# Layer 2 of a four-layer graph kernel: phi1 applied to the features before the sum over neighbours, psi and phi1 taken from the turned h in three exact passes

## The chip, the cores and the metric

The kernel runs on one core of one Trainium2 chip, in one launch. The metric is device time in microseconds (us) from start to end of the execution. TensorE is called PE, VectorE DVE, ScalarE ACT, GpSimd POOL, and SP is the queue that issues nearly all DMAs. PEld is the loading of weights into PE, which overlaps its matmuls.

## The reference

The input is 32 samples (`x`: 32 x 512 nodes x 128 features, float32) with one 512 x 512 adjacency matrix. Four layers follow one another, each as `x = x + layer(relu(layernorm(x)))`. The change lies in layer 2:

```python
h = jnp.maximum(_layernorm(x, axis=-1), 0.0)
weights = coeff * A                       # both are adj here: adj squared
features = relu(einsum('bnd,de->bne', h, psi_w) + psi_b)
messages = einsum('nm,bnd->bmd', weights, features)
phi_in = concatenate((messages, h), axis=-1)
hid = relu(einsum('bnk,kd->bnd', phi_in, phi1_w) + phi1_b)
x = x + einsum('bnd,de->bne', hid, phi2_w) + phi2_b
```

`phi1_w` has 256 rows: the upper 128 meet the messages, the lower 128 meet `h`. Layer 3 is an attention with `tanh`, `exp` and a mask; layers 0 and 1 also mix over the nodes.

## The kernel before

All of `x` stays in SBUF, as 16 pairs of samples. For each sample of a layer, ACT writes the normalised `h` (four instructions of 128 x 128, `chunk`), DVE turns it in 32 x 32 blocks (`turn_half`), and SP sends each pair through DRAM and back (`fetch`), which gives `hT`: features on partitions, nodes along the free axis.

Precision: a product that must be exact in float32 is either a plain float32 matmul (two PE instructions in the profile) or three float32r matmuls of `high`, `low` and `mid` parts. The parts are made by `moving_parts` (ACT, POOL and DVE, from SBUF), `fixed_parts` (ACT, POOL, ACT, POOL, for weights) or `bank_parts` (ACT, then two DVE instructions, straight from a PSUM bank).

Layer 2 is a loop over the samples n = 0 to 31 in `layers_2_and_3`. Each engine works through its instructions in the order in which the program issues them; the order is written out by hand (a manual schedule), so the place of a call in the loop is its place in the queue of every engine it uses. Before the change, iteration n holds, in this order:

- `messages(n)`: 12 float32r matmuls of the feature parts with the squared adjacency (L1182), into bank `p_msgT`.
- `turn_ready`: DVE turns of the h that were written an iteration earlier (one of layer 2, one of layer 3 for n from 8 on), and their stores to DRAM.
- `chunk(3, ...)` for n from 7 on and `chunk(2, n + 7)` for n up to 24: ACT writes h of layer 3 and of layer 2 (L1133). So both come in iterations 7 to 24.
- a DVE scaling of `p_msgT` into `msgT` (L1319), and `biased(n)`: POOL adds `phi2_b` to x (L1209).
- `features(n + 2)`: psi as eight float32 instructions (`p_feat`, L454), bias on DVE (L1170), relu on ACT (L1171), and the three parts (L420 ACT `high`, L421 POOL `low`, L422 DVE `mid`).
- `hidden(n - 1)`: phi1 in float32, two instructions for h (L1191) and two for the messages (L1192), then ACT's relu (L1193).
- `updated(n - 2)`: phi2 in float32 (`p_l2`, in the profile `p_l<-phi,msgT`, L454), DVE adds it to x (L1201). After every second sample, `ln_stats` follows: four DVE statistics (L245), one ACT square root (L252), two short DVE instructions (L256, L257). They serve layer 3.
- in iterations 2 to 5 one more `ln_stats`, for the last pairs of layer 2 (ACT L254).

The last four steps of layer 1 (`mix`, PE line L1027) are interleaved with the first steps of layer 2 by `more(3)` to `more(7)`; there stand `features(0)` and `features(1)`.

`bank` hands out the 8 PSUM banks, `small_tile` 13 SBUF tiles of 128 x 512, `matrix_tile` 3 tiles of 128 x 4 x 512.

Of the kernel before, what the change touches and what calls it, by code (L numbers as in the profile page):

```python
# [9 lines left out]
F32 = mybir.dt.float32  # L10
F32R = mybir.dt.float32r
F16 = mybir.dt.float16
BF16 = mybir.dt.bfloat16
AF = mybir.ActivationFunctionType
# [3 lines left out]
P = 128  # L18
# [11 lines left out]
def kernel(  # L30
# [53 lines left out]
    def bank(name):  # L84
        return psum.tile([P, 512], F32, tag="bank", name=name)

    def tiles(ap):
        return ap.rearrange("p (t f) -> p t f", f=D)

    def blk(t):  # L90
        return slice(t * P, (t + 1) * P)
# [5 lines left out]
    def matrix_tile(name, dtype=F32):  # L97
        return const.tile([P, NT, N], dtype, tag="matrix", name=name, bufs=3)
# [4 lines left out]
    def small_tile(name, dtype=F32):  # L103
        return after.tile([P, N], dtype, tag="small", name=name, bufs=13)

    def crossed(ap):

        return ap.rearrange("p (a b c) -> p b a c", a=NT, b=NQR)

    def split(ap):  # L110
        return ap.rearrange("p (a b c) -> p a b c", a=NT, b=NQR)
# [25 lines left out]
    def load_rows(ap, name, pool=const):  # L137
        o = ap.shape[0] // P
        w = pool.tile([P, o, ap.shape[1]], F32, name=name, bufs=1)
        nc.sync.dma_start(w, ap.rearrange("(o f) g -> f o g", f=P))  # L140
        return w

    def load_bcast(ap, name, pool=const):
        w = pool.tile([P, D], F32, name=name, bufs=1)
        nc.sync.dma_start(w, bass.AP(tensor=ap.tensor, offset=ap.offset, ap=[[0, P], [1, D]]))
        return w

    def spread(w, n):
        return w[:, None, :].to_broadcast([P, n, D])
# [15 lines left out]
        load_x(b)  # L165
    th = load_rows(theta, "th")
    b1 = load_bcast(bias_l1, "b1")
    psi = load_rows(psi_w, "psi")[:, 0, :]
    psib = load_bcast(psi_b, "psib")
    phi1 = load_rows(phi1_w, "phi1")  # L170
    phi1b = const.tile([P, 1], F32, name="phi1b")
    nc.sync.dma_start(phi1b, phi1_b.rearrange("(p o) -> p o", o=1))
    phi2 = load_rows(phi2_w, "phi2")[:, 0, :]
# [235 lines left out]
    def three(name):  # L409
        return [small_tile(f"{part}_{name}", F32R) for part in PARTS]  # L410
# [7 lines left out]
    def moving_parts(x, high, low, mid):  # L418

        nc.scalar.activation(high, x, AF.Copy, scale=DOWN)  # L420
        nc.gpsimd.tensor_sub(low, x, high.bitcast(F32))  # L421
        nc.vector.scalar_tensor_tensor(mid, x, 1.0 / UP, high.bitcast(F32), OP.mult, OP.subtract)  # L422

    def fixed_parts(x, high, low, mid):

        nc.scalar.activation(high, x, AF.Copy, scale=DOWN)
        nc.gpsimd.tensor_sub(x, x, high.bitcast(F32))
        nc.scalar.activation(low, x, AF.Copy, scale=LOW)
        nc.gpsimd.tensor_sub(mid, high.bitcast(F32), low.bitcast(F32))
# [16 lines left out]
    def columns(xT):  # L446
        return lambda t: xT[:, blk(t)]

    def projected(name, *terms):

        p = bank(name)
        for t in range(NT):
            for i, (hT, w) in enumerate(terms):
                nc.tensor.matmul(p[:, blk(t)], hT(t), w, start=(i == 0),  # L454
                                 stop=(i == len(terms) - 1))
        return tiles(p)
# [701 lines left out]
    def hT_of(layer, n):  # L1158
        return hTs[layer, n // 2][:, :, n % 2, :]

    feats, msgT, keys, query, hvs, exs = {}, {}, {}, {}, {}, {}

    def features(n):

        if n >= B:
            return
        hT = hT_of(2, n)
        pf = projected(f"p_feat_{n}", (lambda t: hT[:, t, :], psi))
        feat = small_tile(f"feat_{n}")
        nc.vector.tensor_add(tiles(feat), pf, spread(psib, NT))  # L1170
        nc.scalar.activation(feat, feat, AF.Relu)  # L1171
        feats[n] = three(f"feat_{n}")
        moving_parts(feat, *feats[n])

    def messages(n):

        if n % 4 == 0:
            msgT[n // 4] = matrix_tile(f"msgT_{n}")
        p = bank(f"p_msgT_{n}")
        for part in range(3):  # L1180
            for t in range(NT):
                nc.tensor.matmul(p, feats[n][part][:, blk(t)], sq[part][:, t, :],  # L1182
                                 start=(t == 0 and part == 0), stop=(t == NT - 1 and part == 2))
        return p

    def hidden(n):

        if not 0 <= n < B:
            return
        msg, p = msgT[n // 4][:, n % 4], bank(f"p_phi1_{n}")  # L1190
        nc.tensor.matmul(p, phi1[:, 1, :], hT_of(2, n), start=True, stop=False)  # L1191
        nc.tensor.matmul(p, phi1[:, 0, :], msg, start=False, stop=True)  # L1192
        nc.scalar.activation(crossed(msg), split(p), AF.Relu, bias=phi1b)  # L1193

    def updated(n):

        if not 0 <= n < B:
            return
        q, b = divmod(n, 2)
        p = projected(f"p_l2_{n}", (columns(msgT[n // 4][:, n % 4]), phi2))  # L1200
        nc.vector.tensor_add(xt[q][:, b], p, xt[q][:, b])  # L1201
        if b == 1 and q < NQ - 1:
            ln_stats(q, low=True)
# [90 lines left out]
    def layers_2_and_3():  # L1294


        later, ready = iter(range(B)), [(2, 6)]

        def ahead_of_3():
            m = next(later, B)  # L1300
            if m < B:
                chunk(3, m)
                ready.append((3, m))

        def turn_ready(now):
            for layer, m in now:
                turn_half(layer, m)

        mask_of = adjT_d.rearrange("(a b c) w -> b a c w", a=NT, c=QR)
        for n in range(B):  # L1310
            p = messages(n)
            turn_ready(ready)
            ready = []
            if 7 <= n < B - 1:
                ahead_of_3()
            if n + 7 < B:
                chunk(2, n + 7)
                ready.append((2, n + 7))
            nc.vector.tensor_scalar(msgT[n // 4][:, n % 4], p, UP, None, OP.mult)  # L1319
            biased(n)  # L1320
            features(n + 2)
            if n == B - 1:
                queries(0)
            hidden(n - 1)
            updated(n - 2)
            if n == 0:
                fetch(2, 2)
            elif n % 2 and n + 5 < B:
                fetch(2, n // 2 + 3)
            if n in (2, 3, 4, 5):  # L1330
                ln_stats(NQ - 6 + n)
            if n == 12:
                weights_of_3()
            if n == 20:
                adjTx.append(matrix_tile("adjTx"))
            if n >= 20 and n % 2 and n < 28:
                i = (n - 20) // 2
                tc.keep_in_program_order(nc.sync.dma_start(adjTx[0][:, i, :], mask_of[i]))
            if n in (26, 28, 30):
                fetch(3, (n - 26) // 2)  # L1340
            if n in (29, 30):
                key_parts(n - 29)
        key_parts(2)
        hidden(B - 1)
        mapped(0)
        updated(B - 2)
        updated(B - 1)
        for n in range(B):
            last = n == B - 1
            queries(n + 1)  # L1350
            if n:
                key_parts(n + 2)
            if n == 1:
                low_stats(NQ - 1)
            if last:
                attended(n - 2, NT // 2)
            else:
                scores(n)
                if n == B - 2:
                    attended(n - 1, 0, NT // 2)  # L1360
                    mapped(n + 1)
                    scores(n + 1)
                    continue
            attended(n - 1)
            mapped(n + 1)
            if n % 2:
                turn_ready(ready)
                ready = []
            elif n:
                ahead_of_3()  # L1370
            if n % 2 == 0:
                fetch(3, n // 2 + 3)
        attended(B - 1, width=1)
# [27 lines left out]
    def more(step):  # L1401

        if step == 0:
            chunk(2, 0)
            chunk(2, 1)
        elif step == 1:
            turn_half(2, 0)
        elif step == 2:
            turn_half(2, 1)
            fetch(2, 0)  # L1410
        elif step == 3:
            chunk(2, 2)
        elif step == 4:
            turn_half(2, 2)
            chunk(2, 3)
        elif step == 5:
            turn_half(2, 3)
            fetch(2, 1)
            features(0)
            chunk(2, 4)  # L1420
        elif step == 6:
            features(1)
            turn_half(2, 4)
            chunk(2, 5)
        elif step == 7:
            turn_half(2, 5)
            chunk(2, 6)
# [45 lines left out]
```

## Time and profile before

| | before |
|---|---|
| median of 3 runs | 905.54 us (905.1 to 905.81) |
| the profiled execution, its own time | 905.41 us |
| its span, first to last instruction | 903.6 us |
| granted TensorE clock | 1.0 |
| PE busy | 891.2 us (99%) |
| DVE, ACT, POOL busy | 707.0 (78%), 569.5 (63%), 579.7 (64%) |
| layer 2 on PE, first to last matmul of it | about 433 to 647 us |

The span is 1.8 us shorter than the time of the same execution; that remainder is outside what the trace covers. Busy shares are averages over four layers with different limits. In the timelines, a row is a run of equal instructions: start, duration from the first start to the last end, engine, line, operation, result<-operands, count, and in brackets how long the engine had been idle before and what released it. The end of a matmul is modelled and reaches into the next one, so what a group of matmuls costs PE is read from start to next start.

### The profile page before, as it was taken

The numbers are of one execution on the slowest core, as the hardware profiler recorded it, in microseconds if no ns is written. First come the engines' busy times: TensorE is split into PE (matmuls) and PEld (weight loads), VectorE is DVE, ScalarE is ACT, GpSimd is POOL, SyncE is SP. The second block draws the span as 40 slices with busy tenths as digits, with TensorE's granted clock in tenths as the row PEclk, the third lists the DMA queues.
The fourth block names the chain that finished last, engine by engine and source line by source line (L and its number), as shares of the span: only waits on it lengthen the run. The fifth ranks groups of instructions, "written<-read, shape, count | busy, mean of one in ns | idle before, by whom it ended". The sixth has DMA issues, their size and how long they took to land.

```text
span 903.6 us, 15432 instructions
## 1 busy us (share of the span) xinstructions
PE 891.2 (99%) x5304; PEld 761.8 (84%) x5305; DVE 707.0 (78%) x1476; ACT 569.5 (63%) x1286; POOL 579.7 (64%) x500
## 2 busy tenths in 40 slices
PE   8999999999999999999999999999999999999998
PEld 4899999988888888888876777777789999999998
DVE  7888887569687868788677777777698888987775
ACT  5874554365556655556655877876677777666664
POOL 5877999966867776786344455555476555566653
PEclk9999999999999999999999999999999999999999
DMA  9255644123322221313332444455212223222211
GB/s 256 56 168 160 187 122 114 32 83 83 104 61 82 69 72 48 94 48 94 89 98 71 107 127 140 120 148 154 70 52 79 82 82 105 68 71 74 59 36 48
DMA packets 83919, 86.08 MB, mean 95 GB/s; under 512 B 6784, under 2 KB 74624, under 8 KB 83840
## 3 DMA queue, kind: packets, MB, share of 16 engines
q1 hardware_dynamic: 83552, 84.57, 32.9%
q8 instruction: 42, 0.69, 0.4%
q10 hardware_dynamic: 288, 0.52, 0.2%
q14 instruction: 37, 0.30, 0.1%
HBM read 44.17 MB, written 40.89 MB: 94 GB/s over the span
## 4 chain that ended last, share of the span: by engine, by line
PE 84%; DVE 5%; ACT 4%; POOL 3%; issue 2%; DMA 1%; SPq 1%; DVEq 0%; POOLq 0%; ACTq 0%
PE p_av L1274 12%; PE p_l L1027 9%; PE p_score L1252 9%; PE p_x1T L405 9%; PE p_msgT L1182 6%; PE p_w L1006 5%; PE p_l_c L393 4%; PE p_l_a L393 3%; PE p_l_d L393 3%; PE p_g L454 3%; PE p_hv L454 3%; PE p_w L1008 3%; PE p_l L454 2%; PE p_query L1225 2%; PE p_phi L1191 2%; PE p_phi L1192 2%
## 5 line engine op out<-in xcount | busy, mean ns | idle before, releaser
L1274 PEld LDWEIGHTS p_av<-hv,ex 128*128 128x128 f32 x1024 | 119.3, 191 | 3.5 <-POOL ex L1247 0.8
L421 POOL TENSOR_TENSOR low_feat<-feat,high_feat 128x512 fp32r<-128x512 f32 x32 | 55.7, 1740 | 103.0 <-ACT high_feat L420 103.0
L1274 PE MATMUL p_av<-hv,ex 128*128 128x129 f32 x1024 | 119.8, 274 | 0.6 <-POOL ex L1247 0.6
L435 POOL TENSOR_TENSOR key<-key 128x512 fp32r<-128x512 f32 x32 | 50.0, 1563 | 98.1 <-DVE key L434 39.8
L285 ACT ACTIVATE h<-x,sh,rs 128x128 f32<-128x128 f32 x256 | 102.1, 483 | 11.9 <-DVE sh L257 11.0
L1247 DVE TENSOR_TENSOR ex<-ex,adjTx 128x512 f32<-128x512 f32 x64 | 80.6, 1260 | 35.6 <-ACT ex L1245 33.9
L1247 POOL TENSOR_TENSOR ex<-ex,adjTx 128x512 f32<-128x512 f32 x64 | 98.2, 1553 | 12.3 <-ACT ex L1245 8.1
L1133 ACT ACTIVATE h<-x,sh,rs 128x128 f32<-128x128 f32 x256 | 102.8, 485 | 0.0
L245 DVE BATCH_NORM_STATS2 bn<-x 128x6 f32<-128x256 f32 x244 | 86.1, 418 | 0.0
L421 POOL TENSOR_TENSOR low_h<-h,high_h 128x512 fp32r<-128x512 f32 x32 | 54.6, 1705 | 47.7 <-PE p_w L1008 28.6
L1245 ACT ACTIVATE ex<-ex 128x512 f32<-128x512 f32 x128 | 78.8, 650 | 0.0
L1253 ACT ACTIVATE ex<-p_score 128x512 f32<-128x512 f32 x128 | 73.9, 604 | 1.4 <-PE p_score L1252 1.1
L439 ACT ACTIVATE high_query<-p_query 128x512 fp32r<-128x512 f32 x32 | 19.2, 600 | 73.7 <-PE p_query L1225 73.7
L422 DVE SCALAR_TENSOR_TENSOR mid_feat<-feat,high_feat 128x512 fp32r<-128x512 f32 x32 | 25.5, 798 | 44.3 <-ACT high_feat L420 44.3
L254 ACT ACTIVATE sd<-bn,eps 128x8 f32<-128x8 f32 x46 | 14.0, 305 | 62.7 <-DVE bn L245 58.6
L421 POOL TENSOR_TENSOR low_hs<-hs,high_hs 128x512 fp32r<-128x512 f32 x32 | 44.4, 1399 | 14.2 <-ACT high_hs L420 13.8
L407 ACT COPY x1T<-p_x1T 128x512 f32<-128x512 f32 x32 | 18.8, 586 | 52.2 <-PE p_x1T L405 52.2
L1252 PE MATMUL p_score<-high_query,key 128*128 128x512 f32 x128 | 50.6, 395 | 0.0
L1252 PE MATMUL p_score<-low_query,key 128*128 128x512 f32 x128 | 50.4, 394 | 0.0
L1252 PE MATMUL p_score<-mid_query,key 128*128 128x512 f32 x128 | 50.3, 393 | 0.0
L1008 PE MATMUL p_w<-th,x1T 128*128 128x128 f32 x256 | 49.0, 272 | 0.0
L454 PEld LDWEIGHTS p_l<-phi,msgT 128*128 128x128 f32 x256 | 33.0, 191 | 18.3 <-issue 10.5
(230 smaller groups left out, 2560.8 us busy)
## 6 DMA issues: line engine op xcount, KB each, us to landing
d<-hb SPq DMA_DIRECT2D x128, 128.0 KB, 2.4
hT<-d SPq DMA_DIRECT2D x32, 512.0 KB, 3.4
d_hT<-hb_hT SPq DMA_DIRECT2D x112, 128.0 KB, 2.4
hT<-d_hT SPq DMA_DIRECT2D x28, 512.0 KB, 3.4
x<-in_x_dram SPq DMA_DIRECT2D x32, 256.0 KB, 5.1
out_dram<-x SPq DMA_DIRECT2D x31, 256.0 KB, 2.3
adjT_d<-adj_squares SPq DMA_DIRECT2D x4, 256.0 KB, 4.5
adj_crossed<-in_adj_dram SPq DMA_DIRECT2D x4, 256.0 KB
```

Of the source, the lines that this page charges most:

```text
L245: nc.vector.bn_stats(st[:, k].rearrange("p e s -> p (e s)"), xt[q][:, b, t : t + 2, :].rearrange("p t f -> p f t"))
L285: nc.scalar.activation(h[:, b, t, :], xt[q][:, b, t, :], AF.Relu, bias=shift[q][:, i : i + 1], scale=scale[q][:, i : i + 1])
L393: nc.tensor.matmul(p[:, i * 2 * D : (i + 1) * 2 * D], a[:, k, blk(i)], b[:, k], start=(first and i == 0 and k == 0), stop=(k == 1), skip_g ...
L405: nc.tensor.matmul(p, right[part][:, blk(t)], left[part][:, t, :], start=(t == 0 and part == 0), stop=(t == NT - 1 and part == 2))
L421: nc.gpsimd.tensor_sub(low, x, high.bitcast(F32))
L454: nc.tensor.matmul(p[:, blk(t)], hT(t), w, start=(i == 0), stop=(i == len(terms) - 1))
L1027: nc.tensor.matmul(p, adj_parts[part][:, t, blk(i)], w[r][part][:, t, :], start=(part == 0 and t == 0), stop=(part == 2 and t == NT - 1))
L1133: nc.scalar.activation(h[:, t, :], xt[q][:, b, t, :], AF.Relu, bias=shift[q][:, i : i + 1], scale=scale[q][:, i : i + 1])
L1245: nc.scalar.activation(ex[:, t, :], ex[:, t, :], AF.Exp, scale=8.0)
L1247: eng.tensor_mul(split(ex[:, t, :]), split(ex[:, t, :]), crossed(mask[:, t, :]))
L1252: nc.tensor.matmul(p, keys[n][i][:, t, :], query[n][i], start=(i == 0), stop=(i == 2))
L1274: nc.tensor.matmul(po[:, i, : D + 1], ex[:, t, blk(i0 + i)], hv[:, t, :], start=(t == 0), stop=(t == NT - 1))
```

## The change

Four things change in layer 2.

- **The order of the products.** The features are first multiplied by the upper half of phi1 (`weighed_by_phi`: a float32 product, `p_z`), and the result is what is summed over the neighbours (`summed`). `fixed_parts` and `bank_parts` do the splitting: the parts now come from the bank `p_z`, by `bank_parts`.
- **One bank for phi1.** The product of the lower half of phi1 with h opens a bank (`p_hidden`), and the sum over neighbours is added into that same bank; ACT's relu reads it with a scale (`relu_of`). The DVE scaling of the messages and the tile `msgT` are gone.
- **psi and phi1 on the turned h.** `hT` itself is split into three parts (`split_hT`: two POOL instructions, one DVE), and psi and the lower phi1 are three float32r matmuls each, with the weights stationary and hT moving (`opened`). The features so come out turned, with the bias per partition, and the relu on ACT reads the bank directly; the DVE addition of the bias is gone. The weights are split once (`weights_of_2`).
- **The places in the loop.** An iteration n holds `opened(n + 1)`, the turns and chunks, `split_hT(n + 2)`, `summed(n)`, `biased(n)`, `relu_of(n)`, `weighed_by_phi(n + 1)`, `updated(n - 1)`. Ahead of the loop, `more(3)` holds `weights_of_2` and `split_hT(0)`, `more(4)` `opened(0)`, `more(5)` `weighed_by_phi(0)`, `more(6)` `split_hT(1)`.

```diff
@@ -165,9 +165,11 @@
         load_x(b)
     th = load_rows(theta, "th")
     b1 = load_bcast(bias_l1, "b1")
-    psi = load_rows(psi_w, "psi")[:, 0, :]
-    psib = load_bcast(psi_b, "psib")
-    phi1 = load_rows(phi1_w, "phi1")
+    w2 = const.tile([P, 3, D], F32, name="w2")
+    nc.sync.dma_start(w2[:, 0:2, :], phi1_w.rearrange("(o f) g -> f o g", f=P))
+    nc.sync.dma_start(w2[:, 2, :], psi_w)
+    psib = const.tile([P, 1], F32, name="psib")
+    nc.sync.dma_start(psib, psi_b.rearrange("(p o) -> p o", o=1))
     phi1b = const.tile([P, 1], F32, name="phi1b")
     nc.sync.dma_start(phi1b, phi1_b.rearrange("(p o) -> p o", o=1))
     phi2 = load_rows(phi2_w, "phi2")[:, 0, :]
@@ -1158,46 +1160,75 @@
     def hT_of(layer, n):
         return hTs[layer, n // 2][:, :, n % 2, :]
 
-    feats, msgT, keys, query, hvs, exs = {}, {}, {}, {}, {}, {}
-
-    def features(n):
+    turned_parts, features, sums2, weighed_features, hidden = {}, {}, {}, {}, {}
+    psi_parts, phi_parts = [], []
+    keys, query, hvs, exs = {}, {}, {}, {}
+
+    def weights_of_2():
+
+        pair = small_tile("w2_high", F32R), small_tile("w2_low", F32R)
+        parts = pair[0][:, : 2 * D], pair[0][:, 2 * D :], pair[1][:, : 2 * D]
+        fixed_parts(w2[:, 1:3, :].rearrange("p k f -> p (k f)"), *parts)
+        phi_parts.extend(part[:, :D] for part in parts)
+        psi_parts.extend(part[:, D:] for part in parts)
+        nc.gpsimd.tensor_scalar(psib, psib, 1.0 / UP, 1.0, OP.mult, OP.mult)
+
+    def split_hT(n):
 
         if n >= B:
             return
         hT = hT_of(2, n)
-        pf = projected(f"p_feat_{n}", (lambda t: hT[:, t, :], psi))
-        feat = small_tile(f"feat_{n}")
-        nc.vector.tensor_add(tiles(feat), pf, spread(psib, NT))
-        nc.scalar.activation(feat, feat, AF.Relu)
-        feats[n] = three(f"feat_{n}")
-        moving_parts(feat, *feats[n])
-
-    def messages(n):
-
-        if n % 4 == 0:
-            msgT[n // 4] = matrix_tile(f"msgT_{n}")
-        p = bank(f"p_msgT_{n}")
-        for part in range(3):
+        turned_parts[n] = three(f"hT2_{n}")
+        high, low, mid = (part.rearrange("p (t n) -> p t n", t=NQR) for part in turned_parts[n])
+        nc.gpsimd.tensor_scalar(high, hT, DOWN, 1.0, OP.mult, OP.mult)
+        nc.gpsimd.tensor_sub(low, hT, high.bitcast(F32))
+        nc.vector.scalar_tensor_tensor(mid, hT, 1.0 / UP, high.bitcast(F32), OP.mult, OP.subtract)
+
+
+
+    def opened(n):
+
+        if n >= B:
+            return
+        p = bank(f"p_feat_{n}")
+        for i in range(3):
+            nc.tensor.matmul(p, psi_parts[i], turned_parts[n][i], start=(i == 0), stop=(i == 2))
+        s = sums2[n] = bank(f"p_hidden_{n}")
+        for i in range(3):
+            nc.tensor.matmul(s, phi_parts[i], turned_parts[n][i], start=(i == 0), stop=False, skip_group_check=True)
+        features[n] = small_tile(f"feat_{n}")
+        nc.scalar.activation(features[n], p, AF.Relu, bias=psib)
+
+    def weighed_by_phi(n):
+
+        if n >= B:
+            return
+        p = projected(f"p_z_{n}", (columns(features[n]), w2[:, 0, :])).rearrange("p t f -> p (t f)")
+        if n:
+            z = matrix_tile(f"z_{n}", F32R)
+            weighed_features[n] = [z[:, i] for i in range(3)]
+        else:
+            weighed_features[n] = three(f"z_{n}")
+        bank_parts(p, *weighed_features[n])
+
+    def summed(n):
+
+        for i in range(3):
             for t in range(NT):
-                nc.tensor.matmul(p, feats[n][part][:, blk(t)], sq[part][:, t, :],
-                                 start=(t == 0 and part == 0), stop=(t == NT - 1 and part == 2))
-        return p
-
-    def hidden(n):
-
-        if not 0 <= n < B:
-            return
-        msg, p = msgT[n // 4][:, n % 4], bank(f"p_phi1_{n}")
-        nc.tensor.matmul(p, phi1[:, 1, :], hT_of(2, n), start=True, stop=False)
-        nc.tensor.matmul(p, phi1[:, 0, :], msg, start=False, stop=True)
-        nc.scalar.activation(crossed(msg), split(p), AF.Relu, bias=phi1b)
+                nc.tensor.matmul(sums2[n], weighed_features[n][i][:, blk(t)], sq[i][:, t, :], start=False,
+                                 stop=(i == 2 and t == NT - 1), skip_group_check=True)
+
+    def relu_of(n):
+
+        hidden[n] = small_tile(f"hidden_{n}")
+        nc.scalar.activation(crossed(hidden[n]), split(sums2[n]), AF.Relu, bias=phi1b, scale=UP)
 
     def updated(n):
 
         if not 0 <= n < B:
             return
         q, b = divmod(n, 2)
-        p = projected(f"p_l2_{n}", (columns(msgT[n // 4][:, n % 4]), phi2))
+        p = projected(f"p_l2_{n}", (columns(hidden[n]), phi2))
         nc.vector.tensor_add(xt[q][:, b], p, xt[q][:, b])
         if b == 1 and q < NQ - 1:
             ln_stats(q, low=True)
@@ -1308,7 +1339,7 @@
 
         mask_of = adjT_d.rearrange("(a b c) w -> b a c w", a=NT, c=QR)
         for n in range(B):
-            p = messages(n)
+            opened(n + 1)
             turn_ready(ready)
             ready = []
             if 7 <= n < B - 1:
@@ -1316,13 +1347,14 @@
             if n + 7 < B:
                 chunk(2, n + 7)
                 ready.append((2, n + 7))
-            nc.vector.tensor_scalar(msgT[n // 4][:, n % 4], p, UP, None, OP.mult)
+            split_hT(n + 2)
+            summed(n)
             biased(n)
-            features(n + 2)
+            relu_of(n)
             if n == B - 1:
                 queries(0)
-            hidden(n - 1)
-            updated(n - 2)
+            weighed_by_phi(n + 1)
+            updated(n - 1)
             if n == 0:
                 fetch(2, 2)
             elif n % 2 and n + 5 < B:
@@ -1341,9 +1373,7 @@
             if n in (29, 30):
                 key_parts(n - 29)
         key_parts(2)
-        hidden(B - 1)
         mapped(0)
-        updated(B - 2)
         updated(B - 1)
         for n in range(B):
             last = n == B - 1
@@ -1409,17 +1439,20 @@
             turn_half(2, 1)
             fetch(2, 0)
         elif step == 3:
+            weights_of_2()
             chunk(2, 2)
+            split_hT(0)
         elif step == 4:
             turn_half(2, 2)
+            opened(0)
             chunk(2, 3)
         elif step == 5:
             turn_half(2, 3)
             fetch(2, 1)
-            features(0)
+            weighed_by_phi(0)
             chunk(2, 4)
         elif step == 6:
-            features(1)
+            split_hT(1)
             turn_half(2, 4)
             chunk(2, 5)
         elif step == 7:
```

## The prediction

> **What bounds the kernel now.** I read the page first. Its first part gives PE 99% of the span, so PE sets the time almost everywhere, and a change of PE's work counts in full unless PE starts to wait.
>
> ```profile
> PE 891.2 (99%) x5304; PEld 761.8 (84%) x5305; DVE 707.0 (78%) x1476; ACT 569.5 (63%) x1286; POOL 579.7 (64%) x500
> ```
>
> Next the timeline of PE alone in the middle of layer 2. It shows one sample: subtract each start from the next.
>
> ```profile
> 545.17 1.05 PE L454 MATMUL p_feat<-psi,hT 128*128 128x128 f32 x8
> 546.06 1.02 PE L1191 MATMUL p_phi<-hT,phi 128*128 128x512 f32 x2
> 546.92 1.02 PE L1192 MATMUL p_phi<-msgT,phi 128*128 128x512 f32 x2
> 547.77 1.05 PE L454 MATMUL p_l<-phi,msgT 128*128 128x128 f32 x8
> 548.59 1.18 PE L1182 MATMUL p_msgT<-sq_high,high_feat 128*128 128x512 f32 x4
> ...
> 551.47 1.05 PE L454 MATMUL p_feat<-psi,hT 128*128 128x128 f32 x8
> ```
>
> That is 0.89 for psi, 0.86 and 0.85 for the halves of phi1, 0.82 for phi2, 2.88 for the sum (2.79 in the chain of waits, 0.2325 a matmul): 6.30 us. From the first p_msgT (440.58) to that of sample 31 (635.77) are 195.2 us; the work, 28 samples of 6.29 and 14.4 at both ends, is 190.5. So PE already loses some 4.7 us, nearly all between 475 and 517.
>
> Then ACT alone, over two samples. A square root comes every second sample.
>
> ```profile
> 548.48 0.30 ACT L252 ACTIVATE sd<-bn,eps_low 128x8 f32<-128x8 f32 x1 [2.12 <-DVE bn L245]
> 548.69 3.18 ACT L1133 ACTIVATE h<-x,sh,rs 128x128 f32<-128x128 f32 x8
> 551.78 0.61 ACT L1171 ACTIVATE feat<-feat 128x512 f32<-128x512 f32 x1
> ...
> 552.96 0.67 ACT L1193 ACTIVATE msgT<-p_phi,phi1b 128x512 f32<-128x512 f32 x1
> 553.53 3.19 ACT L1133 ACTIVATE h<-x,sh,rs 128x128 f32<-128x128 f32 x8
> ...
> 557.46 0.63 ACT L420 ACTIVATE high_feat<-feat 128x512 fp32r<-128x512 f32 x1
> ...
> 560.78 0.30 ACT L252 ACTIVATE sd<-bn,eps_low 128x8 f32<-128x8 f32 x1 [2.12 <-DVE bn L245]
> ```
>
> ACT is never idle but before the square root, and everything behind that waits with it. The root waits for DVE, in the whole timeline of the pair before:
>
> ```profile
> 545.82 0.69 DVE L422 SCALAR_TENSOR_TENSOR mid_feat<-feat,high_feat 128x512 fp32r<-128x512 f32 x1 [1.36 <-ACT high_feat L420]
> 546.43 0.68 DVE L1201 TENSOR_TENSOR x<-p_l,x 128x512 f32<-128x512 f32 x1
> 547.03 1.42 DVE L245 BATCH_NORM_STATS2 bn<-x 128x6 f32<-128x256 f32 x4
> ```
>
> So there is a **ring** outside PE: root, two samples of ACT work, `high`, then DVE's mid, x and bn, then the root again. It turns in 560.78 - 548.48 = **12.30 us for two samples; PE needs 12.58**. PE leads by only 0.28. This is what decides the case.
>
> **What the Trainium skill says.** "FP8 and Floating Point Precision", TensorE Precision Notes: true FP32 takes 4 passes through the array. The trace agrees nearly: 0.86 us against 0.2325 for 512 columns, 3.7 to 1, so three exact passes (0.70) beat one float32 product by 0.16. "TensorE: Matmul & The Clock Gate", architectural detail: ACT and DVE are strict FIFO. The trace agrees: the h behind the root start 0.21 after it. "SBUF — State Buffer", two separate sides: DVE and GpSimd share a port pair under an exclusive lock. The trace agrees: at 452.27 low took 1.27 and the mid beside it 1.81; elsewhere mid 0.69 and low 1.79.
>
> **The change part by part.**
>
> *PE work.* psi: 0.89 goes, 3 x 0.2325 = 0.70 comes. Lower phi1: 0.86 to 0.70. Upper phi1: two wide instructions become eight narrow ones, 0.86 both ways, as in phi2. The sum (2.79) and phi2 (0.85) stay. 0.70 + 0.70 + 2.79 + 0.86 + 0.85 = 5.90 a sample against 6.29: 32 x 0.39 = **-12.5** (11 to 13.5, as the switches of type cost 0 to 0.05).
>
> *DVE and POOL counts.* DVE: the bias and the scaling go (0.67, 0.65), z low and z mid come (as low_query and mid_query: 0.68 each): equal. POOL gains one instruction of 0.62 (as L1388): 0.62 + 1.3 to 1.8 + 1.43 = at most 3.9 of 5.9 us, and split_hT runs a whole iteration before `opened` needs it: nothing. Without that cover, `opened` would wait for low.
>
> *The ring.* ACT's queue in iteration n becomes: relu of feat n + 1, the h, relu_of(n), high of z n + 1, root; DVE's: turns, mid of hT, z low, z mid, x, bn. Against the 12.30: relu_of now stands before the last `high` instead of after it, +0.57 (552.96 to 553.53); one more DVE step between high and bn, z mid, +0.60; two relus now read PSUM, start to start about 0.50 instead of 0.65, and high too, -0.37 in all. **13.10 us for two samples, against 11.80 on PE.** The relu that feeds `p_z` and the high that feeds the sum both stand behind the root, so PE waits: 1.30 for each of the nine pairs in iterations 7 to 24, where both kinds of h come. **+11.7** (6 to 15: half if ACT runs ahead; more if the PSUM reads gain nothing). The split of qk in iteration 12 adds 0.3.
>
> *Iterations 2 to 6.* One kind of h only, but roots in each. One root: 0.21 + 0.50 + 1.55 (four h) + 0.57 + 0.60 + three DVE steps 1.80 + bn 1.43 + hand-overs 0.1 = 6.76, or 0.86 over 5.90. Two roots (iterations 2 and 4): 2.12 more, the time from 467.68 to 469.81 in ACT's rows. 3 x 0.86 + 2 x 2.98 = 8.5, less some 0.9 of lead at the start: **+7.6** (4 to 9). In iterations 25 to 31 the ring is 3.1 us shorter and PE leads: nothing.
>
> *The start.* `weights_of_2` is ACT, POOL, ACT, POOL, then psib, then split_hT(0), all needed by `opened(0)` right behind the first mix, at 430.38. The same chain in layer 1:
>
> ```profile
> 180.30 0.72 POOL L427 TENSOR_TENSOR th<-th,th_high 128x256 f32<-128x256 f32 x1
> 181.06 0.42 ACT L428 ACTIVATE th_high<-th 128x256 fp32r<-128x256 f32 x1 [3.50 <-POOL th L427]
> 181.55 0.73 POOL L429 TENSOR_TENSOR th_low<-th_high 128x256 fp32r<-128x256 f32 x1 [0.53 <-ACT th_high L428]
> ```
>
> POOL is busy with L1021 until 429.59; 1.98 for the chain gives 431.57; psib 0.55 (as L272); high 0.62; low 1.3 to 1.8: 434.0 to 434.5. PE wants low 0.23 after its start: **+3.7** (2.5 to 4.5). DVE's mid of hT stands before the eviction of that mix, so the turns and the fetch of pair 1 (landing 442.3) come about 4.7 later, at 447; split in 2.3, at 449.3, where PE reaches `opened(2)` about then: 0 to 0.5, taken as 0. Queues of SP carry the same number of DMAs; the weight loads lie in the first 50 us.
>
> *PSUM.* `p_hidden` lives over an iteration, one bank more. If it had to wait for the relu of two samples before, PE would lose at most what ACT is late, 1.3 a pair, and that is the ring's wait, counted already: 0 taken, 1.3 a pair kept for the range.
>
> *Stalls of before.* The 4.7 us came from the same ring, behind the roots of iterations 2 to 5, and its share is counted anew above: **-4.7** (3 to 4.7). Layer 3 follows PE and moves as a whole: its samples take 7.94 on PE before and after.
>
> **Sum:** -12.5 + 11.7 + 0.3 + 7.6 + 3.7 - 4.7 = **+6.1**. The profiled execution took 905.41 (span 903.6 and 1.8 around it), the median is 905.54, so 911.5 on the one and 911.6 on the other.
>
> **The rivals.** *The ring has slack* (ends faster): if DVE takes x and bn of an earlier sample before z is ready, the root comes early and the ring falls below 11.8. It decides where the ring loses 1.3 us. Then only the two iterations with two roots still cost, 2 x 2.98: 905.4 - 12.5 + 3.7 + 6.0 - 4.7 = 897.9. For it: ACT idles 2.12 at every root, and PE yet lost little. Against: bn needs x, x stands behind z mid in DVE's queue, and z mid behind high. Chance 0.10. *Half of it*: a ring of 12.5, so 0.7 a pair, and 6 in the early iterations: 905.4 - 12.5 + 6.3 + 6.0 + 3.7 - 4.7 = 904.2. Chance 0.12. *The port pair*: POOL's two new reads of hT meet DVE inside the ring once a pair, 1.1 us each (mid's longest 1.83 against 0.69): +10, 921. For it: low alone took 1.79 nearly always. Against: z low and z mid read PSUM, and low_query at 640.17 took 0.69 with POOL busy. Chance 0.13. *My forecast*: 0.65.
>
> **How the numbers follow.** 0.2% (1.8 us, about what a measurement of this kernel tells from no change) makes the band 903.7 to 907.3. My case alone spans 906 to 917. Taking in the half case and half of the port pair gives 902 to 919, and leaves out the slack (0.10) and half of the port pair (0.06). Slower: 0.61 of mine, 0.13 of the port pair, 0.02 of the half case, 0.76; same: 0.04 and 0.07, 0.11; faster: 0.10 and 0.03, 0.13.
>
> **What would show it.** Right: ACT's root rows some 13.1 us apart in iterations 8 to 24 with about 3.4 us idle before them, PE's rows alternately 5.9 and 7.2 apart, PE waits for ACT at `p_z` and at the sum of over 15 us in all, a wait of 3 to 4 us for POOL at 430. Wrong: roots under 12 us apart, PE starts 5.9 apart throughout, or waits of PE for POOL or DMA in the loop.

## The result and the profile after

The changed kernel took **916.39 us** (median of 4 runs, 914.25 to 917.51) against 905.32 (904.95 to 905.81) beside it: 1.0119 times as long, 95% interval 1.01 to 1.0139. It is slower, as forecast, by 11.1 us instead of the 6.1 of the sum. Its profiled execution took 916.19, of which the span is 914.1; before, the span was 903.6. So 10.5 us of span have to be found.

The page of the changed kernel comes first: busy times, the clock that PE was granted in 40 slices, and the chain that ended last by engine.

```profile
PE 890.4 (97%) x5368; PEld 775.5 (85%) x5369; DVE 708.1 (77%) x1476; ACT 566.3 (62%) x1288; POOL 589.9 (65%) x535
...
PEclk9999999999999999999899999999999999999999
...
PE 75%; ACT 11%; DVE 7%; POOL 3%; issue 2%; DMA 1%; SPq 1%; POOLq 0%; DVEq 0%; ACTq 0%
```

PE's busy time is as good as unchanged (891.2 before), though the change took work from it, and its share fell from 99% to 97%. Both say that PE now waits or runs slowly. The single 8 in the clock row says where to look for the second: the twentieth slice of 22.85 us, 434 to 457.

PE's waits in layer 2 (waiting group, releaser; us in total, times, longest) name the engines:

```profile
PE p_z L456 <- ACT feat L1200: 5.4, 3, 2.7
PE p_hidden L1218 <- ACT z L441: 5.2, 8, 0.7
PE p_feat L1195 <- POOL high_hT L1183: 2.0, 1, 2.0
PE p_feat L1195 <- POOL low_hT L1184: 1.5, 2, 1.4
```

ACT is late at exactly the two places that the prediction named, and POOL at the start. ACT's two totals come to 10.6, where the prediction looked for over 15. But the totals understate: the profile models the end of a matmul, and its rows last longer than the step from one start to the next, so a short wait vanishes in them. The starts are the safer measure. The first instruction of the sum, in PE's timeline:

```profile
544.53 1.21 PE L1218 MATMUL p_hidden<-sq_high,z 128*128 128x512 f32 x4
...
550.61 1.09 PE L1218 MATMUL p_hidden<-sq_high,z 128*128 128x512 f32 x4
...
557.57 1.20 PE L1218 MATMUL p_hidden<-sq_high,z 128*128 128x512 f32 x4 [0.45 <-ACT z L441]
...
563.65 1.10 PE L1218 MATMUL p_hidden<-sq_high,z 128*128 128x512 f32 x4
```

The steps are 6.08, 6.96, 6.08: 13.04 us a pair, where PE's work alone needs 11.96 (twice the mean step of 5.982 in e3_both, an experiment below). The row that waits lists 0.45, but came nearly 1 us late.

The ring itself, in the rows of ACT and DVE of that pair:

```profile
552.51 0.30 ACT L254 ACTIVATE sd<-bn,eps_low 128x8 f32<-128x8 f32 x1 [3.31 <-DVE bn L247]
552.72 0.67 ACT L1200 ACTIVATE feat<-p_feat,psib 128x512 f32<-128x512 f32 x1
553.29 3.18 ACT L1135 ACTIVATE h<-x,sh,rs 128x128 f32<-128x128 f32 x8
556.37 0.67 ACT L1224 ACTIVATE hidden<-p_hidden,phi1b 128x512 f32<-128x512 f32 x1
556.94 0.58 ACT L441 ACTIVATE z<-p_z 128x512 fp32r<-128x512 f32 x1
...
561.64 0.59 ACT L441 ACTIVATE z<-p_z 128x512 fp32r<-128x512 f32 x1
562.26 0.69 DVE L442 SCALAR_TENSOR_TENSOR z<-p_z,z 128x512 fp32r<-128x512 f32 x1 [0.54 <-ACT z L441]
562.87 0.68 DVE L443 TENSOR_TENSOR z<-p_z,z 128x512 fp32r<-128x512 f32 x1
563.47 0.68 DVE L1232 TENSOR_TENSOR x<-p_l,x 128x512 f32<-128x512 f32 x1
564.07 1.43 DVE L247 BATCH_NORM_STATS2 bn<-x 128x6 f32<-128x256 f32 x4
565.54 0.30 ACT L254 ACTIVATE sd<-bn,eps_low 128x8 f32<-128x8 f32 x1 [3.30 <-DVE bn L247]
```

Read it as a closed path: root, relu of `p_feat`, the h of two samples, the last `z` high, then DVE's mid, low, x and bn, and the root again. Root to root is 565.54 - 552.51 = 13.03; ACT stands idle 3.30 of it, and DVE 0.54 ahead of this mid.

### The profile page after: what moved, and what is told of

Read it like the earlier page. It is cut to its first block, busy times and chain, and to the rows that moved or that the text cites. A ratio compares the mean times of both kernels' runs of the same rounds, so it can differ in the third digit from the quotient of the medians.

```text
span 914.1 us, 15607 instructions
## 1 busy us (share of the span) xinstructions
PE 890.4 (97%) x5368; PEld 775.5 (85%) x5369; DVE 708.1 (77%) x1476; ACT 566.3 (62%) x1288; POOL 589.9 (65%) x535
## 4 chain that ended last, share of the span: by engine, by line
PE 75%; ACT 11%; DVE 7%; POOL 3%; issue 2%; DMA 1%; SPq 1%; POOLq 0%; DVEq 0%; ACTq 0%
PE p_av L1305 12%; PE p_l L1029 9%; PE p_score L1283 9%; PE p_x1T L407 9%; ACT h L1135 6%; PE p_w L1008 5%; PE p_l_c L395 4%; PE p_hidden L1218 3%; PE p_l_a L395 3%; PE p_l_d L395 3%; PE p_g L456 3%; PE p_hv L456 3%; PE p_w L1010 3%; PE p_query L1256 2%; DVE bn L247 2%
## 5 line engine op out<-in xcount | busy, mean ns | idle before, releaser
L287 ACT ACTIVATE h<-x,sh,rs 128x128 f32<-128x128 f32 x256 | 102.1, 482 | 11.9 <-DVE sh L259 11.0
L1183 POOL TENSOR_SCALAR high_hT<-hT 128x512 fp32r<-128x512 f32 x32 | 20.5, 641 | 82.7 <-PE p_hidden L1198 25.4
L442 DVE SCALAR_TENSOR_TENSOR z<-p_z,z 128x512 fp32r<-128x512 f32 x31 | 21.4, 692 | 48.4 <-ACT z L441 48.4
L423 POOL TENSOR_TENSOR low_hs<-hs,high_hs 128x512 fp32r<-128x512 f32 x32 | 44.4, 1401 | 14.6 <-ACT high_hs L422 14.2
L1240 POOL TENSOR_TENSOR x<-x,phi2b 128x256 f32<-128x256 f32 x64 | 47.1, 758 | 0.0
```

The lines of the kernel that those rows point to most:

```text
L287: nc.scalar.activation(h[:, b, t, :], xt[q][:, b, t, :], AF.Relu, bias=shift[q][:, i : i + 1], scale=scale[q][:, i : i + 1])
```

## The experiments

The theory: two things outside PE's work cost the time, the ring (ACT's square root, behind which the relu for `p_z` waits) and the start (POOL's parts of hT late), and perhaps a third, PE's clock after waits. The rivals: transfers or POOL's ports in the loop, and the new work itself. Each ratio below is to executions of the kernel before that were timed beside the run. Their medians are 904.72 for e1 to e4, 905.51 for e5 to e8 and 905.32 beside the changed kernel, so differences across these groups can be off by some 0.8 us.

**e1_start** moves `opened(0)`, the first use of the parts of hT, and `weighed_by_phi(0)` after it, one step of layer 1 later each. PE so has one more mix of layer 1 to do (2.8 us) before it needs the parts.

```diff
@@ steps 4, 5 and 6, called by more(4), more(5), more(6) ahead of the loop
             turn_half(2, 2)
-            opened(0)
             chunk(2, 3)
...
             fetch(2, 1)
-            weighed_by_phi(0)
+            opened(0)
             chunk(2, 4)
...
+            weighed_by_phi(0)
             split_hT(1)
```

> Only the start of layer 2 is moved: opened(0) stands one mix of layer 1 later, and weighed_by_phi(0) too. My theory: the changed kernel loses two things around 430 us, the wait of PE for POOL's parts (2.00 + 1.35 us) and, after it, 7 us at a granted clock of 0.56, some 2.9 us. With 2.8 us of other PE work in between, the low part (ready at about 434.2) is late by under 1 us, and the clock stays at 1.0: about -5.5, 911 us. Rival 1: the wait only moves (the mid part of hT still stands before the eviction of the mix on DVE and delays the turns): no gain, 916. Rival 2: the clock drop has nothing to do with the wait: -2.6, 913.8, and the clock is low again in that stretch.

910.25 us; 1.0059 of before (1.0044 to 1.0074), so some 6 less than the changed kernel. The waits for POOL at the start were 2.00 and 1.35; one of 0.85 is left. That is 2.5, and the span fell by 5.6 (908.5). Of these, 5.2 lie ahead of the first sum, which starts at 443.74 instead of 448.98, so some 2.7 of them are not the waits' own length. They show in the clock. Busy times by window (span, PE, PEld, DVE, ACT, POOL with their instructions, PE clock, DMA share, GB/s), first the changed kernel:

```profile
434.00:441.20 7.20, 6.93 (x18) 5.44 (x19) 1.25 (x2) 2.22 (x5) 2.12 (x3) 0.56 0.00 0
441.20:449.00 7.80, 7.80 (x40) 6.44 (x39) 7.21 (x14) 5.67 (x14) 0.00 (x0) 1.00 0.36 96
480.00:492.20 12.20, 9.49 (x44) 7.94 (x44) 8.80 (x22) 4.70 (x11) 4.06 (x6) 0.86 0.19 44
```

then e1_start:

```profile
434.00:441.20 7.20, 6.63 (x33) 5.52 (x34) 5.85 (x12) 3.69 (x9) 2.42 (x3) 1.00 0.29 73
480.00:492.20 12.20, 10.68 (x56) 9.65 (x57) 8.11 (x19) 7.07 (x16) 3.95 (x5) 0.86 0.34 87
```

In the first window PE looks equally busy, 6.93 and 6.63 of 7.20, but did 18 matmuls in the one and 33 (8 of them narrow) in the other, at clocks of 0.56 and 1.00. A busy share doesn't show this, and neither does a list of waits. The second low stretch, 0.86, is in both.

**e2_root** leaves the start alone and takes the root out of the ring: bn stays where it is, and the root and the two steps behind it are issued an iteration later, behind that iteration's chunks.

```diff
+    roots = []
+    def stats_of(q, low=False):
+        steps = stats_steps(q, low)
+        go(steps, NT)          # the four bn
+        roots.append(steps)    # root, rs, sh
-            ln_stats(q, low=True)
+            stats_of(q, True)
-                ln_stats(NQ - 6 + n)
+                stats_of(NQ - 6 + n)
...
                 ready.append((2, n + 7))
+            while roots:
+                go(roots.pop(0))
```

> The changed kernel, with the square root of layer 3's and the late layer 2's statistics (and the two short DVE instructions after it) issued one iteration later, behind the h of that iteration, where its input has long been ready; nothing is added or removed. My theory: the ring root - ACT - z - DVE - root sets 13.03 us for two samples, PE's work is 5.97 a sample. From the first sum (448.98) to the last (650.52) are 201.5 us against 182.8 of work, so 18.7 us of waiting (1.7 of it at a low clock near 489) go: 897.7 us, sums 5.97 apart. Rival 1: the ring is ACT's own work or DVE's, and the root only shows the wait: under 3 us gained, 914. Rival 2: the short DVE instructions now wait for the root in front of the split of hT and z, and a new ring of half the size comes: about 907.

899.0 us (898.11 to 900.22), 0.9936 of before (0.9921 to 0.9951): this one edit gains 17.4 us. ACT's rows:

```profile
549.61 0.69 ACT L1200 ACTIVATE feat<-p_feat,psib 128x512 f32<-128x512 f32 x1 [1.00 <-PE p_feat L1195]
550.20 3.18 ACT L1135 ACTIVATE h<-x,sh,rs 128x128 f32<-128x128 f32 x8
553.28 0.29 ACT L254 ACTIVATE sd<-bn,eps_low 128x8 f32<-128x8 f32 x1
553.48 0.67 ACT L1224 ACTIVATE hidden<-p_hidden,phi1b 128x512 f32<-128x512 f32 x1
```

The root starts without a wait, and ACT's idle time now ends with PE: the direction of waiting has turned round. PE's sums come 5.96 to 6.12 apart in all steps but the first and the last. From the second sum to the last it takes 178.34 us where the changed kernel took 196.00, on the same number of sums. The instructions are the same 15607, the transfers and POOL's work among them, so these alone did not set the 13.03.

**e3_both** joins the two edits.

> Both edits together. My theory: the two losses lie one after the other on PE and add: -18.7 and -5.5, 892 us, clock 1.0 throughout. Rival: the start's delay was absorbed by the waits that the ring made anyway, or the gain of the root edit needs ACT to be early: then the sum is smaller, 896 to 899.

893.84 us (892.4 to 895.21), 0.9878 of before (0.9863 to 0.9892). It beats both kernels, by 10.9 and 22.5 us. Its clock is 1.00 over the whole span, and PE's only wait in layer 2 is

```profile
PE p_feat L1195 <- POOL low_hT L1184: 0.8, 1, 0.8
```

**e4_before_root** puts the edit of e2_root into the kernel before.

> The kernel before, with the same edit of the roots. My theory: its ring (12.30 for two samples) lies just under PE's 12.58, so only the 4.7 us lost between 475 and 517, behind the iterations with two roots, go: 900.6 us. So the root edit is worth 4.7 there and 18.7 in the changed kernel. Rival: these 4.7 come from the stores of h and the turns, not from the roots: 905.

901.88 us (901.22 to 902.43), 0.9963 of before (0.9951 to 0.9976). The stalls between 475 and 517 are gone: the sums span 191.25 us instead of 195.19. So the same edit gains 2.8 there, 3.9 by the sums, where 4.7 was expected, and 17.4 in the changed kernel. A step of 7.18 at 449, which the prediction had counted among its 4.7 of stalls, is the same in both kernels. The ring was there before, almost entirely hidden by PE's longer work.

**e5_fill** tests the clock by itself. The waits at the start stay, but PE gets eight matmuls to do in them whose result nothing reads.

```diff
+    def filler(n):
+        p = bank("p_filler")
+        for _ in range(n):
+            nc.tensor.matmul(p, adj_parts[0][:, 0, blk(0)], adj_parts[0][:, 0, :], start=True, stop=True)
...
+            filler(8)
             opened(0)
```

> The changed kernel with eight matmuls of 128 x 512 (1.86 us, their result is read by nobody) put on PE just ahead of opened(0), where it waits 2.1 us for POOL. Nothing else moves and no data comes earlier. Theory: the low clock after the wait comes from PE having stood still; the two waits together must be broken up, then the 7 us at a granted clock of 0.56 come back to 1.0 and some 2.9 us go: 913.5 us, with the low part's wait of 1.35 unchanged. Rival: the clock falls there for another reason (the kind of matmul, or the 1.35 us wait alone): 916.4 and the same low clock.

914.15 us (913.38 to 915.0), 1.0097 of before (1.0081 to 1.0114). The executions overlap with those of the changed kernel (914.25 to 917.51), so the times alone don't tell the two apart. The traces do: the span is 2.5 shorter, the first sum starts 2.58 earlier, and from it to the last sum both take 201.5 or 201.6. PE's timeline and two windows:

```profile
430.45 2.02 PE L1193 MATMUL p_filler<-adj_high 128*128 128x512 f32 x8
432.62 0.50 PE L1201 MATMUL p_feat<-high_hT,w_high 128*128 128x512 f32 x1 [0.15 <-POOL high_hT L1183]
...
434.46 0.50 PE L1201 MATMUL p_feat<-low_hT,w_high 128*128 128x512 f32 x1 [1.34 <-POOL low_hT L1184]
```

```profile
434.00:441.20 7.20, 6.74 (x33) 5.66 (x34) 3.82 (x8) 3.82 (x9) 2.32 (x3) 1.00 0.00 0
...
471.00:478.00 7.00, 7.00 (x33) 5.89 (x32) 5.30 (x11) 3.69 (x10) 3.29 (x4) 0.79 0.42 133
480.00:492.20 12.20, 9.71 (x51) 7.65 (x50) 9.34 (x26) 5.24 (x13) 5.79 (x7) 1.00 0.28 69
```

The useful matmuls start 0.2 later than in the changed kernel (434.46 against 434.27), and yet the kernel ends sooner: with PE kept occupied, the clock stays at 1.00 after the wait. From the low part to the `p_z` behind the mix, the same matmuls take 4.06 where the changed kernel took 6.83. That is the clock's cost, shown apart from the wait's. Neither the kind of matmul nor the wait of 1.34 by itself lowered the clock here. The later low stretch isn't gone. It moved from behind the long wait of iteration 5 to behind that of iteration 3.

**e6_longer** lengthens the ring: DVE's instruction for the middle part of z is issued twice in the changed kernel.

```diff
         bank_parts(p, *weighed_features[n])
+        nc.vector.tensor_sub(weighed_features[n][2], p, weighed_features[n][0].bitcast(F32))
```

> The changed kernel with the DVE instruction that makes the mid part of z done twice (0.60 us from start to start; same result). Theory (ring): of the two extra instructions in a pair only the one between the last high and the root is on the ring, so roots stand 13.03 + 0.60 = 13.6 us apart, and each single root 0.6 more: 9 pairs and 5 iterations, +8, 924 us. Rival (DVE's load is the limit): both count, 14.2 us apart, +14, 930 us. Rival (PE or ACT is the limit, the root only shows it): +0, 916.

928.29 us (927.85 to 931.33), 1.0258 of before (1.0239 to 1.0276), +11.9 on the changed kernel. ACT's roots:

```profile
558.34 0.30 ACT L254 ACTIVATE sd<-bn,eps_low 128x8 f32<-128x8 f32 x1 [4.04 <-DVE bn L247]
...
572.20 0.30 ACT L254 ACTIVATE sd<-bn,eps_low 128x8 f32<-128x8 f32 x1 [4.03 <-DVE bn L247]
```

They are 13.86 apart, +0.83 a pair, and the idle time before each grew by 0.73. The theory had said 13.6 and 924 us, the rival in which DVE's load is the limit 14.2 and 930, so the total alone lies nearer to the rival. DVE's rows of that pair decide:

```profile
563.38 0.69 DVE L442 SCALAR_TENSOR_TENSOR z<-p_z,z 128x512 fp32r<-128x512 f32 x1 [2.00 <-ACT z L441]
...
568.20 0.69 DVE L442 SCALAR_TENSOR_TENSOR z<-p_z,z 128x512 fp32r<-128x512 f32 x1 [0.43 <-ACT z L441]
```

DVE still stands idle at both mids, waiting for ACT, so its load is not the limit. Two instructions are added a pair, and one counts in full: the one between the last `z` high and bn. It cost more than the 0.60 of an ordinary start-to-start step: it starts 0.71 after the instruction before it, which writes the same tile. The last 0.1 is the step from ACT's relu of `p_hidden` to the last `z` high, 0.67 instead of 0.57. There the first of the two seems to count a little: the last four matmuls of the pair's first sum wait for it (0.4 at most), and the `p_z` that this `high` reads comes some 0.2 later behind the start of the sum. This is read from the rows and not tested.

The sums also take 2.1 longer in iterations 25 to 31, where the theory expected nothing; the part on the prediction comes back to this.

**e7_f32** asks what the three exact passes bring. It is e3_both with psi and the lower half of phi1 as one float32 product each on the turned h; the split of hT and the parts of these weights are gone.

```diff
-        for i in range(3):
-            nc.tensor.matmul(p, psi_parts[i], turned_parts[n][i], start=(i == 0), stop=(i == 2))
+        nc.tensor.matmul(p.rearrange("p (t n) -> p t n", t=NQR), w2[:, 2, :], turned_parts[n], start=True, stop=True)
```

> The kernel with both edits, but psi and the lower phi1 as one float32 matmul of 512 columns each (two PE instructions) on hT itself, so without the splitting of hT and of the weights; their scale is put into the weights. Theory: this separates the exact passes from the rest of the change. Two float32 products take 1.72 us, the six passes 1.47 in the trace, so 5.97 becomes 6.22 a sample, 32 x 0.25 = +8.0, less the 0.8 us that PE waits for the split at the start: 901 us. Rival 1: without the split POOL and DVE have less to do and something still hidden gets shorter: 893 or less. Rival 2: the passes' gain is larger than the rows say (weights hidden better): over 904.

902.37 us (901.54 to 903.37), 0.9964 of before (0.9951 to 0.9977). Its sums are 6.29 to 6.32 apart but for the first and the last step, with no wait of PE: the 6.29 of before. So the other parts of the change, phi1 ahead of the sum among them, together gain PE nothing. The passes bring the whole gain of PE's work: 0.32 a sample in the sums' steps, and against e3_both 8.5 us by the medians, 10.0 by the spans. e4_before_root, which is the kernel before with the same roots, took about as long (901.88).

**e8_longer_free** doubles the same instruction where the root is no longer in the ring.

> The kernel with both edits, with the same doubled DVE instruction as in the other kernel of this set. Theory (ring): with the root out of the way the extra instruction lies beside PE's work: 893.8 plus at most 0.5. Rival (DVE's load is near the limit): DVE gains 19 us in all, some of it shows, 897 or more.

897.65 us (897.22 to 899.14), 0.9915 of before (0.99 to 0.993): +3.8 on e3_both. At most 0.5 was expected, and the rival, DVE's load near its limit, said 897 or more: the rival held. What PE waits for, beside the 0.8 of e3_both:

```profile
PE p_feat L1195 <- DVE mid_hT L1185: 2.7, 4, 0.9
```

Four waits, of 0.9 at most, where DVE's middle part of hT is late: DVE has little slack left. Of 32 added instructions, some 20 us of DVE, 3.8 show; in the ring the same ones cost 11.9.

## Why the prediction was right, and where it fell short

The side and the mechanism were right, and the time lies in the range; the middle was 4.9 too low. By the steps of the sum, in the profiled executions:

| step | predicted | measured | from |
|---|---|---|---|
| PE work | -12.5 | -9.9 | 32 x (6.29 - 5.982), mean step between sums in e3_both 5.982, without the first, one of 6.34 and the last of 4.6 |
| ring, iterations 7 to 24, and the qk split | +12.0 | +9.9 | their 18 steps between sums, 117.6, less 9 x 11.964 |
| iterations 2 to 6 | +7.6 | +6.1 | three late steps, 8.43 + 6.77 + 10.56 - 3 x 5.982, less 1.7 of clock |
| start | +3.7 | +3.35 | the waits of 2.00 and 1.35 |
| stalls of before | -4.7 | -3.9 | e4_before_root, 195.19 - 191.25 |
| low clock | not there | +4.6 | 2.9 after the start, 1.7 behind the wait at 487.33 |
| sum | +6.1 | +10.15 | the spans differ by 10.5 |

**The ring** is the step on which the case turned, and it held: 13.03 root to root where 13.10 was worked out, 3.3 idle before the root where 3.4 was. The experiments show it as the cause, since taking the root out gained 17.4 and lengthening it cost 11.9. The early iterations fit too. The roots of iterations 2 to 5, in ACT's timeline, stand at 470.66, 477.45 and 484.23, 6.79 and 6.78 apart for the predicted 6.76, and two roots stand 2.38 and 2.17 apart for 2.12. The rival in which the ring has slack came to 897.9, close to the 899.0 that e2_root measured when it was given that slack. That is luck: the rival charged 6.0 for the early roots, which e2_root doesn't pay, and lacked the low clock of the start, 2.9, and 2.6 of PE's work. Its condition was false in the kernel as changed. The port pair's sign, waits of PE for POOL in the loop, didn't appear, but for one of 0.17 at 453.

One statement on the ring came out right by a narrow margin only, and not for its reason. For iterations 25 to 31 the prediction has it 3.1 us shorter, so that PE leads. ACT does have 3.1 us less to do there, but the roots still stand 12.02 apart, with 3.3 idle before each:

```profile
629.70 0.30 ACT L254 ACTIVATE sd<-bn,eps_low 128x8 f32<-128x8 f32 x1 [3.31 <-DVE bn L247]
...
636.99 0.69 ACT L1224 ACTIVATE hidden<-p_hidden,phi1b 128x512 f32<-128x512 f32 x1 [1.33 <-PE p_hidden L1218]
...
641.72 0.30 ACT L254 ACTIVATE sd<-bn,eps_low 128x8 f32<-128x8 f32 x1 [3.30 <-DVE bn L247]
```

ACT's relu now waits for PE's sum, so the path closes through PE: root, relu, `p_z`, the rest of PE's sample and the next sum, relu, `z`, DVE, root. It is as long as PE's two samples (11.96) to within 0.06, and has no slack: in e6_longer the roots there stand 12.73 apart, longer by the whole 0.71 of one added instruction.

**PE work** was mis-sized by 2.6: a sample takes 5.98 where 5.90 was the term. The four steps other than `p_feat` are within 0.04 of theirs; `p_feat` takes 0.78 for its three passes, and `p_hidden`, three passes of the same size right behind it, 0.70. The extra 0.08 falls on the first pass after phi2, a float32 product: 0.31 or 0.32 for this step, 0.23 for the next. At 447.59 in the changed kernel, where `p_feat` stands behind a float32r mix, its first step is 0.23 too. The kernel before has the same extra in the sum, which there came behind phi2 (its first row, at 548.59, is in the prediction):

```profile
549.60 1.10 PE L1182 MATMUL p_msgT<-sq_low,low_feat 128*128 128x512 f32 x4
550.53 1.10 PE L1182 MATMUL p_msgT<-sq_mid,mid_feat 128*128 128x512 f32 x4
```

The first four matmuls take 1.01 from start to start, the next four 0.93. So the prediction had read it, as 2.88 for the sum in the rows, and then reckoned with the 2.79 of the chain of waits; the 0.08 went over to `p_feat` and was not saved. Most of this error cancels: in a pair that the ring governs, the time is 13.03 whatever PE needs, so a smaller gain is also a smaller wait. The terms for PE work and for the pairs are off by +2.6 and -2.1, and that is one error, counted once in the total.

**The failing step is a term that isn't there**: what a wait does to PE's clock. The prediction charged a wait at its own length. The four matmuls of a group of the mix after the waits at the start, against a like group later, in PE's timeline of the changed kernel:

```profile
436.57 1.91 PE L1029 MATMUL p_l<-w_high,adj_high 128*128 128x512 f32 x4
438.27 1.91 PE L1029 MATMUL p_l<-w_low,adj_low 128*128 128x512 f32 x4
...
442.93 1.09 PE L1029 MATMUL p_l<-w_low,adj_low 128*128 128x512 f32 x4
443.86 1.10 PE L1029 MATMUL p_l<-w_mid,adj_mid 128*128 128x512 f32 x4
```

One group takes 1.70 from start to start, and 0.93 some six microseconds later. From 434.27 to 441.10 lies work of 3.97 (17 wide matmuls), so 2.9 were lost. Behind the wait of 2.71 at 487.33 another 1.7 went (4.89 for 3.18 of work). The Trainium skill has this: "TensorE: Matmul & The Clock Gate", Part 1, states that the clock falls to half after an idle window of about 3.4 us, and that the window runs free, so that the effect varies from run to run. The trace agrees nearly with the half (0.93 against 1.70 is 0.55) and with the variation: the wait of 2.17 ahead of 471.60, in iteration 3, cost no clock here, and in e5_fill the one of 2.13 in the same place did. It does not bear out the length: the two waits of 2.00 and 1.35 with one matmul between them were enough, and so was the single one of 2.71, and here the measurement decides. The prediction foresaw a wait of 3.7 and put nothing behind it.

Left open: why 2.71 lowered the clock and 2.17 did not, and the 0.35 between the table's sum and the spans. An order in which DVE does x and bn ahead of z wasn't tried.

## What to carry to other kernels

Before taking work off the bounding engine, find the closed path among the other engines that turns beside it, and compare its period with the one that the bounding engine is to have: a lead of 0.28 us in 12.58 was all that hid this one. A tiny instruction that waits for another engine (a square root of 0.30) costs its whole in-order queue the wait, and moving it to where its input is long ready can be worth more than the change itself. Where PE is left waiting for 2 to 3 us, reckon with a slower clock for some microseconds behind it, and look at the granted clock of that stretch, since busy shares and waits don't show it.

## What the runs showed of the hardware beyond expectation

The low clock after a wait cost more than half of the wait again: 2.9 us after waits of 3.35, 1.7 after one of 2.71, and eight filler matmuls in the gap removed the first. The first float32r matmul or matmuls behind a float32 product took 0.08 longer than those behind them, in both kernels. The executions of the changed kernel also lie wider apart (914.25 to 917.51) than those of before (904.95 to 905.81), and the shortest of the four is the one with the highest mean clock, 0.997 against 0.994 in the other three: the share of the clock in the 11.1 us varies from one execution to the next.
